# First loads of four stages spread over three DMA queues in a four-layer vision kernel

## The chip, the cores and the metric

The kernel runs on one core of a Trainium2 chip. The metric is the device time of one execution in microseconds. A core has a matrix engine (TensorE, PE in the profile), a vector engine (VectorE, DVE), a scalar engine (ScalarE, ACT), a general engine (GpSimd, POOL) and an engine that in this kernel only issues transfers (SyncE, SP). SP, ACT and POOL can each issue DMAs; a DMA that an engine issues stands in that engine's instruction order, so it waits for the instructions before it and holds up those behind it.

## The reference

Eight images of 56 by 56 pixels and 192 channels, in float32, pass through four residual layers. Each layer normalizes groups of channels and adds a sublayer's result:

```
x = x + L0(gn(x))   # gated Toeplitz mixing along rows and columns
x = x + L1(gn(x))   # attention in shifted 7x7 windows, 6 heads
x = x + L2(gn(x))   # 192 -> 384, 3x3 depthwise conv, four decaying
                    # running averages, layer norm, 384 -> 192
x = x + L3(gn(x))   # 7x7 depthwise conv, layer norm, MLP 192 -> 768 -> 192
```

Layer 1 rolls the image by three rows and three columns before it cuts it into windows, and rolls the result back. Layers 2 and 3 contain a depthwise convolution each, and every pixel of a channel plane is needed for them.

## The kernel before

The layers run one after the other, and between them the images lie in DRAM: x1[b] is image b after layer 0, x2[b] after layer 1. In SBUF an image has two halves of its rows on 64 partitions each, with three groups of 64 channels side by side.

**Layer 0** makes its gated products first and then mixes rows and columns (layer0_mix). It ends with a projection and a gate (L424 matmul, L429 activation, L445 matmul, L453 addition) and stores each image with L476, two DMAs on SP. When its mixing work is nearly through, it calls loaded(), which opens the pool l1x of layer 1's images (three buffers) and loads images 0 and 1.

**Layer 1** needs the image rolled. rolled() (L585 to L593) does the roll while loading: an image is cut into 18 DMAs, six pieces of rows and columns for each of the three channel groups. The large ones move rows of 53 pixels, 212 bytes, the small ones rows of three pixels, 12 bytes. The same function stores the finished image, rolled back, with 18 more. All are on SP. layer1_norm copies the image into windows and normalizes (ACT L614, PE L621, DVE L623 and following), layer1_scores and layer1_mix do the attention, and DVE's L762 adds the result into the image's own buffer, which is stored from there. Image b+2 is loaded in the middle of image b.

**Layer 2** begins with layer2_in, once per image: two memsets on POOL clear the border rows of the buffer x2 (L769, L770), two DMAs on SP bring the image's halves (L772, L773), DVE normalizes into xn (L778), two memsets on POOL clear xn's border (L781, L782), PE multiplies with w_in (L790), DVE adds b_in (L798), and the result pt goes to DRAM (pd, L799, SP). The pool l2x has two buffers for x2; they lie where layer 1's images lay. w_in and b_in are brought by POOL through the helper resident (L96).

layer2_mix then does the 3x3 convolution over all images at once, a group of channels at a time. For each group it loads a band of weights wt (L820) and one piece zc of every image's pd (L825), all on SP; PE's L834 needs them. convolve does the same for layer 3's 7x7 convolution (wt L997, zc L1002 from zd, PE L1009).

**What sets the order.** A planner orders the instructions of each engine. It goes by the order of the program as priority and by its own estimate of when an instruction can start, so a load may be placed on a queue far ahead of its place in the code if the queue is idle and its buffer is free, and behind one that comes later in the code. On the chip each engine then runs its instructions in that fixed order, and an instruction that waits holds up all behind it. A pool's buffers are used in turn; a new tile's first write waits for the last use of the memory.

Of the kernel before, what the change touches and what calls it, by code (L numbers as in the profile page):

```python
# [10 lines left out]
F32 = mybir.dt.float32  # L11
# [6 lines left out]
B, H, W, C = 8, 56, 56, 192  # L18
# [26 lines left out]
R2 = P2 + 1  # L45
# [31 lines left out]
def kernel(ctx: ExitStack, tc: tile.TileContext, a: dict, out: bass.AP):  # L77
    nc = tc.nc
    nimg = a["x"].shape[0]
# [14 lines left out]
    def resident(name, eng=nc.sync, pool=const):  # L94
        t = pool.tile(list(a[name].shape), F32, name=name + "_sb", bufs=1)
        eng.dma_start(t, a[name])  # L96
        return t
# [29 lines left out]
    x1 = [dram.tile([C, NT], F32, name=f"x1_{b}") for b in range(nimg)]  # L127
# [3 lines left out]
    zd = [dram.tile([OP, C, NB], F32, name=f"zd{b}") for b in range(nimg)]  # L131
# [3 lines left out]
    pd = [dram.tile([128, C2, P2], F32, name=f"pd{b}") for b in range(nimg)]  # L135
# [446 lines left out]
        nc.vector.tensor_scalar(wg[:, :, 0:C], wg[:, :, 0:C], HD ** -0.5, None, ALU.mult)  # L582
        return wg, bq, w_proj, bpr

    def rolled(dram_image, tile_image, store):  # L585

        d = dram_image.rearrange("(j p) (h w) -> p j h w", p=64, w=W)
        for s, h0, h1, r0 in ((0, 0, 28, 3), (1, 0, 25, 31), (1, 25, 28, 0)):
            for w0, w1, c0 in ((0, 53, 3), (53, 56, 0)):
                for j in range(3):  # L590
                    sb = tile_image[64 * s:64 * s + 64, j, h0:h1, w0:w1]
                    dr = d[:, j, r0:r0 + h1 - h0, c0:c0 + w1 - w0]
                    nc.sync.dma_start(dr, sb) if store else nc.sync.dma_start(sb, dr)  # L593

    def layer1_load(b, pool):
        x = pool.tile([128, 3, H // 2, W], F32, name="x1")
        rolled(x1[b], x, False)
        return x

    def layer1_norm(b, x, pool, psum, consts):  # L600
# [161 lines left out]
            nc.vector.scalar_tensor_tensor(xs, ps, bpr[:, j:j + 1], xs, ALU.add, ALU.add)  # L762


    def layer2_in(b, pool, xpool, psum, w_in, b_in):


        x = xpool.tile([128, 3, R2, W], F32, name="x2")
        nc.gpsimd.memset(x[0:64, :, 0], 0.0)  # L769
        nc.gpsimd.memset(x[64:128, :, R2 - 3:R2], 0.0)  # L770
        src = x2[b].rearrange("(j p) (h w) -> p j h w", p=64, w=W)
        nc.sync.dma_start(x[0:64, :, 1:R2], src[:, :, 0:R2 - 1])  # L772
        nc.sync.dma_start(x[64:128, :, 0:R2 - 3], src[:, :, R2 - 1:H])  # L773
        sc, sh = scsh2[:, b, 0], scsh2[:, b, 1]
        xn = pool.tile([128, 3, R2, 64], F32, name="xn2")
        nc.gpsimd.memset(xn[:, :, :, W:64], 0.0)
        for j in range(3):
            nc.vector.tensor_scalar(  # L778
                xn[:, j, :, 0:W], x[:, j], sc[:, j:j + 1], sh[:, j:j + 1], ALU.mult, ALU.add
            )  # L780
        nc.gpsimd.memset(xn[0:64, :, 0, 0:W], 0.0)  # L781
        nc.gpsimd.memset(xn[64:128, :, R2 - 3:R2, 0:W], 0.0)  # L782
        pt = pool.tile([128, C2, P2], F32, name="pt")
        nh = R2 // 2
        for i in range(nh):
            ns = 2 if i + nh < P2 else 1
            ps = psum.tile([128, 2, 512], F32, name="pin")
            for j in range(3):
                for s in range(ns):
                    nc.tensor.matmul(  # L790
                        ps[:, s, 0:C2], xn[64 * s:64 * s + 64, j, 2 * i:2 * i + 2].rearrange("p h w -> p (h w)"),
                        w_in[64 * s:64 * s + 64, j], start=(j == 0), stop=(j == 2),
                    )

            v = 0 if i == 0 else 2 if i + nh == P2 - 1 else 1
            dims = [list(z) for z in pt.ap]
            dst = bass.AP(pt.tensor, pt.offset + i, [dims[0], [nh, ns], [P2, C2]])
            nc.vector.tensor_tensor(dst, ps[:, 0:ns, 0:C2], b_in[:, v, 0:ns], ALU.add)  # L798
        nc.sync.dma_start(pd[b], pt)  # L799

    def layer2_mix():
# [5 lines left out]
        with ExitStack() as st:  # L807
            pool = st.enter_context(tc.tile_pool(reuse_waits="tile", name="mx", bufs=2))
# [8 lines left out]
            def load(g):  # L817
                cs = slice(g * CG2, (g + 1) * CG2)
                wt = pool.tile([128, CG2, 256], F32, name="wt2")
                nc.sync.dma_start(  # L820
                    wt, bass.AP(band.tensor, band.offset + g * CG2 * BL2, [[1, 128], [BL2, CG2], [1, 256]])
                )
                zc = pool.tile([128, nimg, CG2, P2], F32, name="zc2")
                for b in range(nimg):
                    nc.sync.dma_start(zc[:, b], pd[b][:, cs])  # L825
                return wt, zc

            def front(c4, wt, zc, loc, rows, sums):
# [159 lines left out]
    def convolve():  # L988

        band = a["band"]  # L990
        with ExitStack() as st:
            pool = st.enter_context(tc.tile_pool(reuse_waits="tile", name="cv", bufs=2))
            psum = st.enter_context(tc.tile_pool(reuse_waits="tile", name="cvp", bufs=3, space=PSUM))
            for g in range(C // CG):
                cs = slice(g * CG, g * CG + CG)
                wt = pool.tile([OP, CG, BAND], F32, name="wt")
                nc.sync.dma_start(  # L997
                    wt, bass.AP(band.tensor, band.offset + g * CG * BL, [[1, OP], [BL, CG], [1, BAND]])
                )
                zc = pool.tile([OP, nimg, CG, NB], F32, name="zc")  # L1000
                for b in range(nimg):
                    nc.sync.dma_start(zc[:, b], zd[b][:, cs])  # L1002
                yc = pool.tile([OP, nimg, CG, NPAIR], F32, name="yc")
                for c4 in range(0, CG, 4):
                    ps = psum.tile([OP, 2, 512], F32, name="cps")
                    for i in range(4):
                        dst = ps[:, i // 2, 256 * (i % 2):256 * (i % 2) + nimg * NPAIR]
                        for q in range(4):
                            nc.tensor.matmul(  # L1009
                                dst.rearrange("p (b n) -> p b n", n=NPAIR),  # L1010
                                wt[:, c4 + i, q * OP:(q + 1) * OP], zc[:, :, c4 + i, q:q + NPAIR],
                                start=(q == 0), stop=(q == 3),
                            )
                    for j in range(2):
                        src = ps[:, j].rearrange("p (i z) -> p i z", i=2)[:, :, 0:nimg * NPAIR]
                        src = src.rearrange("p i (b n) -> p b i n", n=NPAIR)
                        dst = yc[:, :, c4 + 2 * j:c4 + 2 * j + 2]
                        if j == 0:
                            nc.vector.tensor_copy(dst, src)
                        else:  # L1020
                            nc.scalar.copy(dst, src)
                for b in range(nimg):
                    nc.sync.dma_start(yd[b][:, cs], yc[:, b])
# [94 lines left out]
    with ExitStack() as st:  # L1118
# [6 lines left out]
        x = layer0_load(0, pool)  # L1125
# [28 lines left out]
    with ExitStack() as st:  # L1154
        pool = st.enter_context(tc.tile_pool(reuse_waits="tile", name="mix", bufs=2))
        psum = st.enter_context(tc.tile_pool(reuse_waits="tile", name="mixp", bufs=2, space=PSUM))
        w_p = resident("w_p", nc.gpsimd, pool)
        w_o = resident("w_o", nc.gpsimd, pool)

        ops = [psum.tile([128, 8, H], F32, name=f"op{k}", bufs=1) for k in range(2)]  # L1160
        for op in ops:
            nc.vector.memset(op, 0.0)
        images, x = ExitStack(), []

        def loaded():
            raws.close()
            xpool = images.enter_context(tc.tile_pool(reuse_waits="tile", name="l1x", bufs=3, side="right"))
            x.append(xpool)
            x.extend(layer1_load(b, xpool) for b in range(min(2, nimg)))

        layer0_mix(pool, blocks, psum, ops, w_p, w_o, loaded)


    with ExitStack() as st:
# [22 lines left out]
        xr = [next(steps)]  # L1197
        for _ in steps:
            pass
        values = layer1_scores(0, xr[0], pool, psum, S, es, consts)  # L1200


# [37 lines left out]
    with ExitStack() as st:  # L1240
        xpool = st.enter_context(tc.tile_pool(reuse_waits="tile", name="l2x", bufs=2, side="right"))
        pool = st.enter_context(tc.tile_pool(reuse_waits="tile", name="l2i", bufs=2))
        psum = st.enter_context(tc.tile_pool(reuse_waits="tile", name="l2ip", bufs=4, space=PSUM))
        w_in = resident("w_in", nc.gpsimd, pool)
        b_in = resident("b_in", nc.gpsimd, pool)
        for b in range(nimg):
            layer2_in(b, pool, xpool, psum, w_in, b_in)
            if b == nimg - 3:
                run(gn_finish(mv2[:, last], scsh2[:, last, 0], scsh2[:, last, 1], pool, psum, "pin"))
    layer2_mix()  # L1250
# [168 lines left out]
```

## Time and profile before

| | us |
|---|---|
| median of 3 runs | 6330.82 (6327.23 to 6345.44) |
| profiled execution | 6351.08 |
| its span | 6349.2 |
| PE busy in it | 5569.1 (88%) |
| DVE busy | 3439.3 (54%) |
| ACT busy | 2239.7 (35%) |
| POOL busy | 1302.1 (21%) |
| PE idle before layer 1's first matmul (L621) | 22.01 |
| PE idle before layer 2's first matmul (L790) | 55.65 |
| PE idle before layer 2's convolution (L834) | 27.89 |
| PE idle before layer 3's convolution (L1009) | 22.48 |

All durations come from the one profiled execution. In the lines of a timeline the first number is the start in microseconds from the beginning of the span, the second the time taken; then come the engine, the line of the code, the operation, the tile written and the tiles read, and how many instructions the row sums up. In brackets stands how long the engine had been idle before, and what released it. "SPq" rows are DMA issues on SP: their time is the time at the queue, not that of the transfer. q1 is the queue of SP, q0 that of POOL.

### The profile page before, as it was taken

What the parts mean: (1) busy time and instruction counts of PE and PEld (TensorE: products, weight loads), DVE (VectorE), ACT (ScalarE), POOL (GpSimd) and SP (SyncE); (2) the same over time, 40 slices, a digit from 0 to 9 for tenths busy, and PEclk for the clock granted to TensorE, in tenths of its full rate; (3) what the DMA queues carried; (4) which work ended last, traced back from release to release, by engine and by line L of the source; (5) the groups of instructions that cost most, each with busy time, mean ns of one, the idle gap of its engine ahead of it and who ended that gap; (6) DMA issues with size and microseconds to landing.
All of it is one profiled execution on the core that took longest, in us unless ns stands there. A gap on an engine that the chain in (4) does not pass through costs nothing. (4 is left out here: it accounts for less than half of the span.)

```text
span 6349.2 us, 126376 instructions
## 1 busy us (share of the span) xinstructions
PE 5569.1 (88%) x55636; PEld 3587.9 (57%) x55636; DVE 3439.3 (54%) x4752; ACT 2239.7 (35%) x2922; POOL 1302.1 (21%) x813
## 2 busy tenths in 40 slices
PE   6799989999999688888888598999588798789999
PEld 5677766666666345545445375777244498344444
DVE  5677765555665344444444486888688511532321
ACT  2334444443344233333332102555355300333333
POOL 1100034544444122122121102333110100110100
PEclk8899999999999888888888799999798799899999
DMA  6799886666665613444433675666667488121211
GB/s 166 185 221 210 188 262 263 260 253 240 240 252 194 88 33 55 60 58 63 55 48 44 103 266 208 224 228 233 153 203 208 170 305 305 64 67 56 70 54 27
DMA packets 1039131, 1013.10 MB, mean 160 GB/s; under 512 B 832104, under 2 KB 964372, under 8 KB 1011572
## 3 DMA queue, kind: packets, MB, share of 16 engines
q1 hardware_dynamic: 1028064, 954.17, 53.7%
q0 software_dynamic: 5648, 31.32, 1.5%
q10 hardware_dynamic: 4868, 19.52, 0.9%
q8 instruction: 437, 7.16, 0.5%
q14 instruction: 114, 0.93, 0.0%
HBM read 676.28 MB, written 345.08 MB: 161 GB/s over the span
## 5 line engine op out<-in xcount | busy, mean ns | idle before, releaser
L366 PE MATMUL qv<-w_qv_sb,xn 64*112 64x288 f32 x5376 | 722.2, 425 | 50.9 <-DVE act L372 47.6
L404 POOL COPY lc<-lt 128x896 f32<-128x896 f32 (+1 forms) x320 | 573.0, 1808 | 616.7 <-PE op L412 598.7
L366 PEld LDWEIGHTS qv<-w_qv_sb,xn 64*112 64x112 f32 x5376 | 535.5, 184 | 232.8 <-DVE act L372 64.7
L1087 PE MATMUL ph<-y,w_sb 64*128 64x392 f32 x2304 | 429.9, 511 | 49.1 <-ACT hid L1091 49.1
L373 ACT ACTIVATE act<-act 112x576 f32<-112x576 f32 x448 | 299.5, 682 | 461.7 <-DVE act L372 428.2
L1098 PE MATMUL po<-hid,w_sb 128*64 128x392 f32 x2304 | 395.1, 496 | 10.8 <-ACT hid L1091 10.8
L412 PEld LDWEIGHTS op<-rc,lc 128*56 128x56 f32 x9216 | 308.4, 136 | 127.6 <-issue 65.7
L412 PE MATMUL op<-rc,lc 128*56 128x56 f32 x9216 | 339.7, 222 | 46.0 <-POOL lc L404 24.2
L424 PE MATMUL pj<-xn,w_p_sb 64*128 64x392 f32 (+1 forms) x1920 | 373.0, 515 | 7.7 <-issue 4.7
L445 PE MATMUL y<-pp,w_o_sb 128*64 128x392 f32 (+1 forms) x1920 | 355.9, 503 | 20.4 <-DVE x L453 11.6
L372 DVE TENSOR_TENSOR act<-qv,b_qv 112x576 f32<-112x576 f32 x448 | 320.8, 751 | 86.1 <-PE qv L366 85.7
L1105 DVE TENSOR_TENSOR x<-x,z 128x392 f32<-128x392 f32 x96 | 55.8, 581 | 557.9 <-ACT z L1103 557.9
L1087 PEld LDWEIGHTS ph<-y,w_sb 64*128 64x128 f32 x2304 | 230.5, 194 | 224.1 <-ACT hid L1091 55.2
L404 ACT COPY rc<-rt 128x896 f32<-128x896 f32 (+1 forms) x160 | 256.9, 1606 | 230.7 <-PE op L412 216.0
L834 PE MATMUL cv<-zc,wt 128*128 128x224 f32 x1536 | 312.8, 355 | 27.9 <-DMA zc<-pd 27.9
L834 PEld LDWEIGHTS cv<-zc,wt 128*128 128x128 f32 x1536 | 290.5, 189 | 71.0 <-issue 54.9
L705 POOL TENSOR_TENSOR e<-e,mx 128x1176 f32<-128x1176 f32 x64 | 139.9, 2186 | 925.1 <-DVE mx L704 874.4
L655 PE MATMUL qk_ps<-xr,wg 64*96 64x392 f32 x1536 | 309.6, 511 | 14.9 <-ACT qk L661 13.3
L438 DVE TENSOR_TENSOR pp<-pp,ot 128x784 f32<-128x784 f32 (+1 forms) x160 | 154.6, 967 | 308.4 <-ACT pp L429 287.2
L1009 PE MATMUL cps<-zc,wt 128*128 128x224 f32 x1536 | 299.3, 356 | 23.1 <-DMA zc<-zd 22.5
L1009 PEld LDWEIGHTS cps<-zc,wt 128*128 128x128 f32 x1536 | 290.0, 189 | 32.5 <-issue 24.9
L847 POOL TENSOR_TENSOR rows<-rows,loc 128x896 f32<-128x896 f32 x96 | 228.1, 2377 | 390.2 <-ACT rows L843 262.8
(206 smaller groups left out, 9321.5 us busy)
## 6 DMA issues: line engine op xcount, KB each, us to landing
lt<-left SPq DMA_DIRECT2D x72, 1792.0 KB
rt<-right SPq DMA_DIRECT2D x72, 1792.0 KB
left<-qv SPq DMA_DIRECT2D x224, 252.0 KB
right<-qv SPq DMA_DIRECT2D x448, 126.0 KB
wt<-in_band_dram SPq DMA_DIRECT2D x24, 2048.0 KB
wt<-in_band_dram SPq DMA_DIRECT2D x12, 4096.0 KB
pd<-pt SPq DMA_DIRECT2D x8, 5568.0 KB
zc<-pd SPq DMA_DIRECT2D x192, 232.0 KB
```

The source lines that it names most:

```text
L366: nc.tensor.matmul(ps[s][:, which, 0:D1 // 2], xn[64 * s:64 * s + 64, j, bass.ts(i, 2 * W)], w_qv[64 * s:64 * s + 64, j, which, ns], start ...
L372: nc.vector.tensor_tensor(act, ps[s][:, :, 0:D1 // 2], b_qv[:, :, ns], ALU.add)
L373: nc.scalar.activation(act, act, AF.Silu)
L404: copy(c[:, 0:nu], raw.rearrange("p (w u d) -> p u d w", u=nu, d=64 // nu)[:, :, d0:d0 + 8])
L412: nc.tensor.matmul(op[64 * u:64 * u + W, i, :], lc[:, u, i], rc[:, u, i], start=True, stop=True)
L424: nc.tensor.matmul(ps[0:M, s, 0:TT], w_p[64 * s:64 * s + 64, j, d0:d0 + M], xn[64 * s:64 * s + 64, j, ts], start=(j == 0), stop=(j == 2),)
L445: nc.tensor.matmul(y[64 * s:64 * s + 64], w_o[0:M, c, 64 * j:64 * j + 64], pp[0:M, s], start=(c == gated[0][0]), stop=(c == gated[-1][0]),)
L655: nc.tensor.matmul(ps[s], wg[64 * s:64 * s + 64, j, c0:c0 + HC], xw[64 * s:64 * s + 64, j, gs], start=(j == 0), stop=(j == 2),)
L834: nc.tensor.matmul(dst, wt[:, c4 + i, 128 * q:128 * q + 128], zc[:, :, c4 + i, q:q + NPAIR], start=(q == 0), stop=(q == 1),)
L1009: nc.tensor.matmul(dst.rearrange("p (b n) -> p b n", n=NPAIR), wt[:, c4 + i, q * OP:(q + 1) * OP], zc[:, :, c4 + i, q:q + NPAIR], start=(q ...
L1087: nc.tensor.matmul(ps[:, s, 0:TT], w0[64 * s:64 * s + 64, j, m * 128:(m + 1) * 128], y[64 * s:64 * s + 64, j, ts], start=(j == 0), stop=(j ...
L1098: nc.tensor.matmul(ps[64 * s:64 * s + 64], w1[:, m, 64 * j:64 * j + 64], hid[:, m, s], start=(m == 0), stop=(m == 5),)
```

## The change

rolled and layer1_load take a list of queues and deal the channel groups out over them; layer 1's image 0 uses SP, POOL and ACT, six DMAs each. Image 1 is loaded from a place in the program after image 0's normalization. The first part of layer2_in becomes layer2_image(b, xpool, queue), called one image ahead: image 0's two halves go through POOL, the others through SP. w_in and b_in go through ACT, and image 0's load stands before them. In layer2_mix and convolve, the eight zc pieces of the first group go through SP, POOL and ACT in turn, those of the later groups through SP as before. One more tile of the pool l1x is asked for before image 0's (with eight images, -8 % 3 is 1), and nothing reads or writes it.

```diff
-    def rolled(dram_image, tile_image, store):
+    def rolled(dram_image, tile_image, store, queues=(nc.sync,)):
...
                 for j in range(3):
+                    eng = queues[j % len(queues)]
...
-                    nc.sync.dma_start(dr, sb) if store else nc.sync.dma_start(sb, dr)
+                    eng.dma_start(dr, sb) if store else eng.dma_start(sb, dr)
...
-    def layer2_in(b, pool, xpool, psum, w_in, b_in):
-
+    def layer2_image(b, xpool, queue):
         x = xpool.tile([128, 3, R2, W], F32, name="x2")
         nc.gpsimd.memset(x[0:64, :, 0], 0.0)
         nc.gpsimd.memset(x[64:128, :, R2 - 3:R2], 0.0)
         src = x2[b].rearrange("(j p) (h w) -> p j h w", p=64, w=W)
-        nc.sync.dma_start(x[0:64, :, 1:R2], src[:, :, 0:R2 - 1])
-        nc.sync.dma_start(x[64:128, :, 0:R2 - 3], src[:, :, R2 - 1:H])
+        queue.dma_start(x[0:64, :, 1:R2], src[:, :, 0:R2 - 1])
+        queue.dma_start(x[64:128, :, 0:R2 - 3], src[:, :, R2 - 1:H])
+        return x
+
+    def layer2_in(b, x, pool, psum, w_in, b_in):
...
                 zc = pool.tile([128, nimg, CG2, P2], F32, name="zc2")
+                queues = (nc.sync,) if g else (nc.sync, nc.gpsimd, nc.scalar)
                 for b in range(nimg):
-                    nc.sync.dma_start(zc[:, b], pd[b][:, cs])
+                    queues[b % len(queues)].dma_start(zc[:, b], pd[b][:, cs])
...
-            x.extend(layer1_load(b, xpool) for b in range(min(2, nimg)))
+
+            for _ in range(-nimg % 3):
+                xpool.tile([128, 3, H // 2, W], F32, name="x1")
+            x.append(layer1_load(0, xpool, (nc.sync, nc.gpsimd, nc.scalar)))
...
         xr = [next(steps)]
         for _ in steps:
             pass
+        if nimg > 1:
+            x.append(layer1_load(1, xpool))
         values = layer1_scores(0, xr[0], pool, psum, S, es, consts)
...
-        w_in = resident("w_in", nc.gpsimd, pool)
-        b_in = resident("b_in", nc.gpsimd, pool)
+        x = [layer2_image(0, xpool, nc.gpsimd)]
+        w_in = resident("w_in", nc.scalar, pool)
+        b_in = resident("b_in", nc.scalar, pool)
         for b in range(nimg):
-            layer2_in(b, pool, xpool, psum, w_in, b_in)
+            if b + 1 < nimg:
+                x.append(layer2_image(b + 1, xpool, nc.sync))
+            layer2_in(b, x[b], pool, psum, w_in, b_in)
```

convolve is changed like layer2_mix.

More of the change, by code (lines that the diff above doesn't have):

```diff
@@ L590, in rolled, with layer1_load @@
                 for j in range(3):
+                    eng = queues[j % len(queues)]
                     sb = tile_image[64 * s:64 * s + 64, j, h0:h1, w0:w1]
                     dr = d[:, j, r0:r0 + h1 - h0, c0:c0 + w1 - w0]
-                    nc.sync.dma_start(dr, sb) if store else nc.sync.dma_start(sb, dr)
-    def layer1_load(b, pool):
+                    eng.dma_start(dr, sb) if store else eng.dma_start(sb, dr)
+    def layer1_load(b, pool, queues=(nc.sync,)):
         x = pool.tile([128, 3, H // 2, W], F32, name="x1")
-        rolled(x1[b], x, False)
+        rolled(x1[b], x, False, queues)
         return x
@@ L1000, in convolve @@
                 zc = pool.tile([OP, nimg, CG, NB], F32, name="zc")
+                queues = (nc.sync,) if g else (nc.sync, nc.gpsimd, nc.scalar)
                 for b in range(nimg):
-                    nc.sync.dma_start(zc[:, b], zd[b][:, cs])
+                    queues[b % len(queues)].dma_start(zc[:, b], zd[b][:, cs])
                 yc = pool.tile([OP, nimg, CG, NPAIR], F32, name="yc")
```

## The prediction

> **What bounds the kernel now.** I read the page first, then the order of work on each queue around the four places that the diff touches, then the DMA engines in the same windows. In the page, TensorE (PE) is busy for 88% of the span:
>
> ```profile
> span 6349.2 us, 126376 instructions
> PE 5569.1 (88%) x55636; PEld 3587.9 (57%) x55636; DVE 3439.3 (54%) x4752; ACT 2239.7 (35%) x2922; POOL 1302.1 (21%) x813
> ```
>
> A change to loads can only win back time in which PE stands. In PE's timeline (start, length, line, tile, count, and in brackets the idle time before and what ended it) the four places are these four gaps:
>
> ```profile
> 2127.05 3.61 PE L621 MATMUL mean<-xr,ones 128*128 128x392 f32 x5 [22.01 <-issue]
> ...
> 3613.33 2.29 PE L790 MATMUL pin<-w_in_sb,xn 64*128 64x384 f32 x6 [55.65 <-POOL xn L781]
> ...
> 3884.49 1.83 PE L834 MATMUL cv<-zc,wt 128*128 128x224 f32 x4 [27.89 <-DMA zc<-pd]
> ...
> 5071.99 1.46 PE L1009 MATMUL cps<-zc,wt 128*128 128x224 f32 x3 [22.48 <-DMA zc<-zd]
> ```
>
> I call them A (into layer 1), B (into layer 2), C and D (first group of each convolution). Together 22.0 + 55.7 + 27.9 + 22.5 = 128 us, 2.0% of the span: the ceiling of the change. What fills A and B is seen in SP's queue:
>
> ```profile
> 2058.78 53.81 SPq L593 DMA_DIRECT2D x<-x  x36
> 2112.69 1.24 SPq L476 DMA_DIRECT2D x<-x  x2
> 2113.98 2.62 SPq L593 DMA_DIRECT2D x<-x  x1
> ...
> 3555.74 38.40 SPq L593 DMA_DIRECT2D x<-x  x18
> 3594.68 0.59 SPq L772 DMA_DIRECT2D x<-x  x1
> 3596.91 0.59 SPq L773 DMA_DIRECT2D x<-x  x1
> 3598.85 0.57 SPq L772 DMA_DIRECT2D x<-x  x1
> ```
>
> and in what the other engines wait for:
>
> ```profile
> 2126.21 5.83 ACT L614 ACTIVATE xr<-x,scsh 128x392 f32<-128x392 f32 x9 [33.01 <-DMA x<-x]
> 2126.22 2.69 POOL L1192 MEMSET e<- 128x1536 f32 x2 [24.77 <-DMA x<-x]
> ...
> 3560.57 0.26 POOL L769 MEMSET x<- 64x168 f32 x1
> 3598.84 0.23 POOL L769 MEMSET x<- 64x168 f32 x1 [37.45 <-DMA x<-x]
> 3609.71 3.28 DVE L778 TENSOR_SCALAR xn<-x,scsh 128x1680 f32<-128x1680 f32 x3 [50.34 <-DMA x<-x]
> 3613.05 0.23 POOL L781 MEMSET xn<- 64x168 f32 x1 [13.43 <-DVE xn L778]
> ```
>
> In A, ACT and POOL, which share nothing but reused memory, are released in the same moment, 12.3 us after the L476 store's last issue (2113.93): what they wait for is the store of layer 0's last image, not image 0's load. That store was ready about 2099, when DVE had made its last values, and stood behind 36 loads of images 0 and 1. In B the chain is: 18 stores of image 7, the two halves of layer 2's image 0, DVE, POOL's small memset L781, PE. The two L769 lines matter most: x2(0)'s memset did not wait, x2(1)'s waited 37.45 us for image 7's stores. So image 7 already lies outside layer 2's first buffer and inside its second.
>
> **Is it issue or bandwidth?** The DMA engines between 2058 and 2113 (busy tenths in 40 slices, then packets), and the first queue's share between 3857 and 3885 (C):
>
> ```profile
> DMA  0399999669999998723179999989999999994932
> ...
> DMA packets 43554, 5.97 MB, mean 109 GB/s; under 512 B 43374, under 2 KB 43374, under 8 KB 43550
> q1 hardware_dynamic: 43326, 4.82, 88.6%
> ...
> q1 hardware_dynamic: 3884, 10.24, 97.2%
> ```
>
> A moves slowly (109 GB/s) but its engines are full of packets under 512 B; C runs at 370 GB/s on full engines. D (5051 to 5072) likewise gave 361 GB/s at 100.5%, and B's stores 89.3% with 11.0% for b_in.
>
> **What the Trainium skill says.** The page "DMA: Bandwidth & Descriptors", section "Issuing engines are not separate DMA queues", says that DMAs begun on SP, ACT or GpSimd run on the same 16 engines and interleave, and that several issuers save only sequencer time; the shares above agree. Its section "SWDGE vs HWDGE vs iDMA" says that each engine takes turns between its queues; the trace agrees in B, where b_in on POOL's queue landed 9.9 us after its issue while the older stores nearly stood. "Rules for kernel authors" says that two halves of the partitions use the same engines and serialize: so x2's two halves are costed as one transfer.
>
> **Part A.** Image 0's 18 loads become 6 each on SP, POOL and ACT; image 1's are written after layer 1's first normalization, behind the store in program order. But the planner issues on an idle queue whatever is ready: in the trace SP issued image 2's first load at 2113.98, though the code has it half an image later. I therefore expect SP to carry 6 loads, image 1's 18 and one or so of image 2 before the store is ready. One load costs 53.81 / 36 = 1.49 us on average, a large one (1,792 rows; 24 ns for such a packet, over 16 engines) 2.7 us. Removed: the issue-bound ends, six small loads per image at 0.61 us, of which perhaps half finds other traffic: 2 x 3.7 / 2 = 3.7 us. Added: one large load, 2.7 us. Gain 1.0 us, taken. Ends: if image 1's loads do stay behind, the store starts between 2100 and 2107 and lands 13 us later, so ACT begins 5 to 13 us sooner; if three or four of image 2 slip ahead, 5 us are lost. ACT's 6 issues stand among the gate's L429 activations, which feed PE; the trace has no DMA of ACT there. At 1.49 us they cost 9 us of ACT, hidden while the last values arrive before the store's turn, 2112.7 against 2099: cover 13.7 us. At the largest issue on SP (5.6 us) they would take 34 us, and then A is lost by about 10. I take nothing. POOL is idle from 2058.75 to 2092.55, which covers its 6 issues unless they take over 34 us; the nearest rows, POOL issues of 49 to 384 descriptors, took 0.53 to 0.76 us.
>
> **Part B.** Layer 2's image 0 is written first and loads from POOL's queue; w_in and b_in move to ACT, image 1 stays on SP behind the stores. POOL reached x2(0)'s memset at 3560.57, after L776, whose memory comes free with DVE's last L762 (3558.5); I expect the same, since x2(0)'s and x2(1)'s memsets were queued one after the other, as if all of layer 1's buffers came free at once. The load then starts at about 3561 among the stores. It is 2.35 MB in 384 packets of 515 ns: 384 x 515 / 16 = 12.4 us of all engines. DVE's 3 x 3.28 = 9.8 us could follow at about 3575. But POOL is in order: x2(1)'s two memsets, waiting for image 7's stores, stand ahead of L781 and L782, which wait for DVE, and PE waits for L781. So PE starts when the stores have landed: 3598.84 + 12.4 (full engines, x2(0) served among them) + 0.75 (x2(1)'s memsets) + 0.3 (L781) = 3612.3, against 3613.33: 1.0 us gained. The stores' last, smallest transfers may leave gaps that take some of the 12.4, so I take 2. Ends: nothing absorbed and w_in (0.59 MB, at C's 370 GB/s 1.6 us) moved among the stores, loss 1; half of 12.4 absorbed, gain 7. Image 1 does not add a stall: its load lands about 14 us after the stores, plus 9.8 of DVE, within image 0's 30.5 us on PE.
>
> **Part C and D.** C moves, in turn, the pd store (14.1 us), the weights (5.9) and eight zc (5.3), all of which PE's first matmul needs, at 97.2% of the engines: three issuers change their order and not the sum. SP's blocked issue (20.98 us for eight) only waited for the pd store. Gain 0; ends -2 (the second group's weights, no longer held back by SP, share the engines with the last zc) and +1. D: weights 10.8 us and zc 5.6 at 100.5%; only the first 3 us (5051.4 to 5054.9) could start sooner. I take 0.5; ends 0 and 3.
>
> **The unread tile.** One extra tile per three images shifts the order of layer 1's buffers, if a tile that nothing reads or writes counts at all. I take it as without effect: image 7 stays where the L769 lines show it.
>
> **Sum.** 1.0 + 2.0 + 0 + 0.5 = 3.5 us less in a profiled execution of 6351.08 us (span 6349.2), which lay 20.3 above the median of the runs; the same difference against the median gives 6330.8 - 3.5 = 6327.3 us. No change under 0.3% (19 us) can be told from none in this kernel.
>
> **Rivals.** *First, the waits really go* (chance 0.37). If L781 stands ahead of x2(1)'s memsets, PE starts at about 3585, computes image 0 in 30.5 us, and then waits for image 1 (stores 3611, load 13, DVE 9.8, so 3634) where it would have begun at 3643.8: 10 gained, up to 20 if x2(0) starts before the stores. With A's 5 to 13: 6330.8 - (15 + 8 + 0.5) = 6307, down to 6290. For it: DVE idles 50 us and nothing but queue order holds L781. Against it: in this trace x2(1)'s and x2(2)'s memsets come before the later L781. *Second, slower* (0.18): the extra tile does count and puts image 7 into x2(0)'s buffer. Then x2(0)'s memset waits for the stores (3598.8); its load is issued at 3600 and shares the engines with x2(1)'s, landing after 2 + 12.4 to 2 + 24.8 us; with 9.8 of DVE and 0.3, PE starts between 3624.5 and 3637, a loss of 11 to 24, time 6342 to 6355, taken as 6349. It decides from a landing at 3622 on. For it: three buffers, and layer 2's first is as wide as one and a bit. Against: nothing uses the tile. *Third, ACT's issues block the gate* (0.07): PE's last layer 0 work ends 10 us later, 6338. *The change hardly does what it says* is the forecast itself (0.38): the bytes and the in-order wait remain.
>
> **Numbers.** Forecast 0.38 at 6327, its own range 6316 to 6340, nearly all within 0.3%. First rival 0.37, of which 0.32 is over 19 us. Second 0.18, of which 0.13 over. Third 0.07, of which 0.03. With 0.01 from the forecast's own ends on each side: faster 0.33, slower 0.17, same 0.50. The range goes from 6292, near the first rival's end, to 6348, and leaves out about a tenth on each side.
>
> **What would show it.** A: on SP some 24 loads ahead of L476, ACT's first L614 at 2120 to 2128. B: x2(0)'s load issued by POOL near 3561, DVE's first L778 near 3575, yet L781 only after a L769 that waits for image 7, near 3611. C and D: the gaps 27.9 and 22.5 within 3 us. Wrong: L781 before that L769, or L476 issued before 2107 (faster); a waiting first L769, or ACT's L429 apart by issues (slower).

## The result, and the profile after

The change makes the kernel slower by a little: 6350.5 us (median of 13 runs) against 6330.8, a ratio of 1.0033 with a 95% interval of 1.0022 to 1.0045. Measured once more later, beside the kernel before on one chip, it was 6352.4 against 6340.6, ratio 1.0019 (1.0011 to 1.0027). So the loss lies near 12 to 20 us. The forecast was 6327.3 us, and its range ended at 6348.

The profiled execution of the change has a span of 6344.6 us, which is shorter than that of the kernel before (6349.2): stages that the change does not touch differ from one execution to the next by as much as the loss. So I compare the stages and not the spans. PE's timeline of the changed kernel, at the four places of the prediction (start, length, line, tile, count, idle time before and what ended it; lines have moved by 1 to 6):

```profile
2122.01 4.26 PE L622 MATMUL mean<-xr,ones 128*128 128x392 f32 x6 [7.92 <-issue]
...
3616.18 24.25 PE L794 MATMUL pin<-w_in_sb,xn 64*128 64x384 f32 x132 [66.87 <-POOL xn L785]
...
3887.56 2.95 PE L839 MATMUL cv<-zc,wt 128*128 128x224 f32 x7 [28.54 <-DMA zc<-pd]
...
5071.72 8.53 PE L1015 MATMUL cps<-zc,wt 128*128 128x224 f32 x33 [20.30 <-DMA zc<-zd]
```

B has grown from 55.65 us to 66.87, by 11.2. C is 0.6 longer, D 2.2 shorter. A seems to have shrunk from 22.0 to 7.9, but that is no gain. PE's last work of layer 0 has moved back. Here are the last gate activation of ACT ahead of layer 1's loads and PE's last row of layer 0, in the kernel before and in the changed one:

```profile
2056.09 0.92 ACT L429 ACTIVATE pp<-pj,vecs_sb 128x784 f32<-128x784 f32 x1 [2.46 <-PE pj L424]
2094.25 2.42 PE L445 MATMUL y<-pp,w_o_sb 64*64 64x392 f32 x12 [1.21 <-DVE pp L438]
...
2048.36 0.92 ACT L429 ACTIVATE pp<-pj,vecs_sb 128x784 f32<-128x784 f32 x1 [2.46 <-PE pj L424]
2102.47 3.98 PE L445 MATMUL y<-pp,w_o_sb 64*64 64x392 f32 x12 [1.21 <-DVE pp L438]
```

ACT's timeline of the changed kernel shows why PE is later ("ACTq" rows are DMA issues on ACT, with the time for which they held it):

```profile
2051.07 10.25 ACTq L594 DMA_DIRECT2D x<-x  x3
2061.43 0.91 ACT L429 ACTIVATE pp<-pj,vecs_sb 128x784 f32<-128x784 f32 x1 [10.93 <-issue]
2061.45 6.05 ACTq L594 DMA_DIRECT2D x<-x  x1
...
2068.55 5.30 ACTq L594 DMA_DIRECT2D x<-x  x2
```

Six issues held ACT for 21.6 us between the gate's activations, which feed PE. The L429 among them is the line to look at: its 10.93 us of idle time end with "issue", not with a result of PE. From one and the same L429 activation, the last one ahead of the loads (2056.09 before, 2048.36 after; called the common L429 below), to PE's first matmul of layer 1 it took 70.96 us before and takes 73.65 now. So A costs 2.7 us more. SP in the meantime:

```profile
2051.06 48.10 SPq L594 DMA_DIRECT2D x<-x  x26
2107.09 1.25 SPq L476 DMA_DIRECT2D x<-x  x2
```

SP was through with 26 loads at 2099.2 and then stood still until the store of layer 0's last image was ready, at 2107.1. Together the four places give 2.7 + 11.2 + 0.6 - 2.2 = 12.3 us.

Layer 2's start holds most of the loss. The queues of SP, POOL and DVE in the changed kernel, and of POOL's two transfers the time from issue to landing (last number, us):

```profile
3547.36 45.94 SPq L594 DMA_DIRECT2D x<-x  x18
3596.02 0.59 SPq L772 DMA_DIRECT2D x<-x  x1
...
3543.92 0.23 POOL L769 MEMSET x<- 64x168 f32 x1
...
3544.67 0.67 POOL L772 DMA_DIRECT2D x<-x  x1
...
3596.12 0.23 POOL L769 MEMSET x<- 64x168 f32 x1 [50.15 <-DMA x<-x]
...
3614.95 1.18 POOL L785 MEMSET xn<- 64x168 f32 x1 [18.04 <-DVE xn L782]
...
3610.54 6.48 DVE L782 TENSOR_SCALAR xn<-x,scsh 128x1680 f32<-128x1680 f32 x6 [59.55 <-DMA x<-x]
```

```profile
x<-x POOLq DMA_DIRECT2D x1, 1218.0 KB, 10.8
...
x<-x POOLq DMA_DIRECT2D x1, 1134.0 KB, 18.5
```

Image 0's halves were issued at 3544.67 and 3545.33 and had landed by 3563.8. Still DVE did nothing until 3610.54, and then ran six normalizations in a row, those of image 0 and of image 1. What came at 3610.5 is image 1's load, issued at 3596.0 behind the stores. In the program's order on DVE, one of image 1's three normalizations stands ahead of image 0's. The lines show it: POOL's L785 waits for image 0's three and was released at 3614.95, when four of the six were done (3610.54 + 4 x 6.48 / 6 = 3614.86). DVE is in order as POOL is: it waited with image 0 ready for 47 us.

### The profile page after: what moved, and what is told of

It is laid out like the page before. It is cut to its first block, busy times and chain, and to the rows that moved or that the text cites. A ratio compares the mean times of both kernels' runs of the same rounds, so it can differ in the third digit from the quotient of the medians.

```text
span 6344.6 us, 126393 instructions
## 1 busy us (share of the span) xinstructions
PE 5564.0 (88%) x55636; PEld 3581.2 (56%) x55636; DVE 3434.6 (54%) x4752; ACT 2239.3 (35%) x2922; POOL 1312.0 (21%) x825
## 5 line engine op out<-in xcount | busy, mean ns | idle before, releaser
L445 PE MATMUL y<-pp,w_o_sb 128*64 128x392 f32 (+1 forms) x1920 | 361.3, 508 | 25.7 <-DVE x L453 11.6
L1015 PE MATMUL cps<-zc,wt 128*128 128x224 f32 x1536 | 298.9, 356 | 20.5 <-DMA zc<-zd 20.3
```

The costliest lines, as they stand in the source:

```text
L445: nc.tensor.matmul(y[64 * s:64 * s + 64], w_o[0:M, c, 64 * j:64 * j + 64], pp[0:M, s], start=(c == gated[0][0]), stop=(c == gated[-1][0]),)
L1015: nc.tensor.matmul(dst.rearrange("p (b n) -> p b n", n=NPAIR), wt[:, c4 + i, q * OP:(q + 1) * OP], zc[:, :, c4 + i, q:q + NPAIR], start=(q ...
```

## The experiments

### Each part alone

Three kernels take one part of the change each, and leave the rest as in the kernel before. The times that the expectations name are counted from the first 6330.8 us; in the comparisons that follow, the kernel before had medians of 6336 to 6342 us, so the differences and ratios are what to compare.

```diff
# a_only: layer 1's loads as in the change; layer 2 as before, and
-  queues = (nc.sync,) if g else (nc.sync, nc.gpsimd, nc.scalar)
+  queues = (nc.sync,)
# b_only: layer 2's loads as in the change, the others as before
# cd_only: the two zc lines as in the change, the others as before
```

> Layer 1's first loads alone: image 0 over three queues, image 1 behind the first normalization, the rest as in the kernel before. Theory: ACT's six issues block for some 20 us between the gate's activations, so PE's last work of layer 0 ends about 15 us later, while SP reaches the store 7 us sooner; PE's first matmul of layer 1 comes 0 to 3 us later, counted from the first load: 6331 to 6335 us. Rival (the missing 10 us of the whole sit here, as a slower layer 1 or a lower clock after the longer gate): 6339 to 6345 us.

> Layer 2's first loads alone: image 0 on POOL's queue, w_in and b_in on ACT's, image 1 on SP's. Theory: DVE has one instruction of image 1 ahead of image 0's, so PE waits for image 1's load: gap of 66 to 68 us before layer 2's first matmul against 55.7, 6340 to 6344 us. Rival (the loss of the whole lies elsewhere): gap as before, 6329 to 6333 us.

> The first loads of both convolutions over three queues, the rest as in the kernel before. Theory: the transfers are limited by the DMA engines; gaps of 28 and 20 to 22 us, 6328 to 6332 us. Rival (three queues at once make the engines slower): gaps longer by 5 us and more, 6336 to 6345 us.

Measured against the kernel before: a_only ratio 1.0007 (0.9999 to 1.0014), about +4 us; from the common L429 to layer 1's first matmul 73.7 us against 71.0. b_only 1.0017 (1.0007 to 1.0026), about +11 us, with a gap of 67.8 us. cd_only 0.9994 (0.9984 to 1.0004), about -4 us and not told from nothing, with gaps of 27.8 and 20.5 us. PE's first matmul of layer 2 in b_only:

```profile
3621.96 38.36 PE L794 MATMUL pin<-w_in_sb,xn 64*128 64x384 f32 x218 [67.78 <-POOL xn L785]
```

The part of layer 2 is most of the loss, as its gap says. A gap alone does not tell what a stage costs, since it also shrinks when the work before it ends late: A's gap is 7.6 us in a_only and 22.0 before, and the kernel is not faster.

### Does the issue on ACT stall the gate?

```diff
-            x.append(layer1_load(0, xpool, (nc.sync, nc.gpsimd, nc.scalar)))
+            x.append(layer1_load(0, xpool, (nc.sync, nc.gpsimd)))
```

on top of a_only.

> Layer 1's first loads alone, as before in this series, but image 0 is dealt out over SP and POOL only, none to ACT. Theory (ACT's blocked issues stall the gate): the gate ends on time, SP is through with its loads about 7 us sooner than in the kernel before, so PE's first matmul of layer 1 comes 5 to 9 us sooner, counted from the first load: 5 to 9 us less than before. Rival (the small descriptors on POOL's queue hold up the engines): no gain against the three-queue form, 0 to 5 us more than before.

Measured: 0.9983 (0.9972 to 0.9994), about 11 us less than before. The stretch from the common L429 to layer 1's first matmul is 62.8 us, 8.2 less than before and 11 less than with ACT. SP and PE:

```profile
2044.00 44.45 SPq L594 DMA_DIRECT2D x<-x  x22
2088.55 5.19 SPq L476 DMA_DIRECT2D x<-x  x2
```

```profile
2104.07 4.26 PE L622 MATMUL mean<-xr,ones 128*128 128x392 f32 x6 [13.89 <-issue]
```

Of image 0's loads, SP has twelve here and POOL six. The store follows directly on the loads before it, of which there are 22 on SP, since eight of image 1's now come after it. POOL's six issues (5.4 us) cost PE nothing; six like them on ACT cost it the gain. The two forms differ in these eight loads too, but in the change SP stood free for 7.9 us ahead of the store, so most of the 11 us between them is put down to ACT's stall.

### Is it the store's place in the queue?

The kernel before, with one line of store() changed, used for the last image:

```diff
+            queue = nc.scalar if b == nimg - 1 else nc.sync
             for s in range(2):
-                nc.sync.dma_start(
+                queue.dma_start(
```

> The kernel before with one change: the store of layer 0's last image is issued by ACT, not by SP behind the 36 loads. Theory (it is the store's place in SP's queue that holds layer 1 back): the store is issued near its readiness, 12 us sooner, its large packets take turns with the small ones, and PE's gap into layer 1 falls from 22 us to 9 to 13: 9 to 13 us less than before. Rival (the engines are full, so the place in the queue does not matter): gap of 19 us and more, 0 to 3 us less.

Measured: 0.9971 (0.9962 to 0.9980), about 18 us less than before, with nothing else of the change in it. SP, ACT and PE of that kernel:

```profile
2055.47 63.29 SPq L595 DMA_DIRECT2D x<-x  x37
```

```profile
2094.00 1.36 ACTq L477 DMA_DIRECT2D x<-x  x2
```

```profile
2109.21 4.26 PE L623 MATMUL mean<-xr,ones 128*128 128x392 f32 x6 [7.51 <-issue]
```

The loads' issues now take until 2118.8, and layer 1 begins 9.6 us before that. The store was issued at 2094.0 and had landed by 2108.4, when POOL was released. The DMA engines were full then as before: from 2094 to 2109, ACT's queue, which held only the store, had 64.0% of them and SP's queue of loads 33.8%. So the place in a queue does matter: on a queue of its own the store took turns with the loads instead of standing behind all of them. Counted from the common L429 it was issued after 41.2 us instead of 56.6, and the whole stretch is 56.4 us against 71.0, a little more gain than the theory's 9 to 13.

### What holds DVE, and what holds POOL?

First try: image 0 of layer 2 issued by ACT instead of POOL, on top of b_only.

```diff
-        x = [layer2_image(0, xpool, nc.gpsimd)]
+        x = [layer2_image(0, xpool, nc.scalar)]
```

> As the run with layer 2's first loads alone, but image 0's two halves are issued by ACT instead of POOL, behind w_in and b_in. The planner then puts image 0's three normalizations first on DVE. Theory (DVE's order is what costs): PE then waits only for POOL's L769, that is for image 7's stores: gap of 49 to 53 us, about 15 us less than with POOL, 6324 to 6330 us. Rival (the load's traffic among the stores is what costs): gap of 65 us and more, 6340 to 6345 us.

Measured: 1.0007 (0.9997 to 1.0016), gap 54.8 us. Neither gap came out. DVE's order was right (image 0's three first), but the load was late. ACT's queue:

```profile
3561.15 0.37 ACTq L96 DMA_DIRECT2D b_in_sb<-in_b_in_dram  x1
3593.93 0.69 ACTq L772 DMA_DIRECT2D x<-x  x1
3596.03 0.61 ACTq L773 DMA_DIRECT2D x<-x  x1
```

The load stood 32 us at the head of ACT's queue, and went out as the last of SP's 18 stores were issued (to 3594.4). In the trace this wait ends with the landing of one of SP's stores, whose completion is counted by the same semaphore as the load's; SP's and ACT's transfers use one set of semaphores in turn in this program. That the load had to wait until the semaphore's last user had landed is the likely cause; I did not try it apart. So this run does not decide between the two theories.

Second try: image 1 goes through POOL's queue as well, behind image 0.

```diff
-                x.append(layer2_image(b + 1, xpool, nc.sync))
+                x.append(layer2_image(b + 1, xpool, nc.sync if b else nc.gpsimd))
```

> Layer 2's first loads alone, with images 0 and 1 both on POOL's queue. The planner then has image 0's three normalizations first on DVE. Theory: DVE is done early and PE waits for POOL alone, whose L785 stands behind the memset and the issues of image 1, that is behind image 7's stores: gap of 49 to 52 us, 4 to 7 us less than before. Rival (the traffic among the stores costs as much as the order): gap of 56 us and more, no gain.

Measured: 1.0019 (1.0011 to 1.0027), about 12 us more than before. In the groups of instructions (busy time, mean ns | idle time before, by releaser):

```profile
L794 PE MATMUL pin<-w_in_sb,xn 64*128 64x384 f32 x1392 | 241.9, 498 | 65.5 <-POOL xn L785 52.7 <-DVE pt L802 12.8
```

The first gap is 52.7 us, near what was expected. A second of 12.8 us has come. SP had sent image 2's load at 3599.01, since image 2 takes image 0's buffer, and POOL sent image 1's at 3605.20, so that the later image moved first. DVE, in order, waited with image 0's additions behind image 1's normalization.

The same with image 0's border left out, so that nothing on POOL follows its normalization:

```diff
+        if b == 0:
+            nc.gpsimd.memset(xn[0:64, :, 0, 0:W], 0.0)
+            nc.gpsimd.memset(xn[64:128, :, R2 - 3:R2, 0:W], 0.0)
         for j in range(3):
+            parts = ((0, 64, 1, R2), (64, 128, 0, R2 - 3)) if b == 0 else ((0, 128, 0, R2),)
+            for p0, p1, r0, r1 in parts:   # tensor_scalar on these rows
...
+        if b:
             nc.gpsimd.memset(xn[0:64, :, 0, 0:W], 0.0)
```

> As the run before it, and image 0's normalization leaves out xn's border rows, which POOL clears beforehand, so that nothing of POOL follows DVE for image 0 (six half instructions of DVE in place of three). Theory: both in-order waits are gone; PE starts 20 to 24 us after layer 1's end, then waits 12 to 18 us for image 1: 15 to 20 us less than before. Rival (the image's load does not land among the stores): first gap of 40 us and more, at most 5 us less.

Measured: 1.0010 (1.0000 to 1.0019), no gain (the interval reaches from none to 12 us more). PE and DVE of that kernel:

```profile
3558.07 5.46 PE L801 MATMUL pin<-w_in_sb,xn 64*128 64x384 f32 x8 [9.91 <-DVE xn L787]
3566.36 19.36 PE L801 MATMUL pin<-w_in_sb,xn 64*128 64x384 f32 x88 [2.83 <-DVE xn L787]
3624.88 25.51 PE L801 MATMUL pin<-w_in_sb,xn 64*128 64x384 f32 x134 [39.17 <-DVE pt L809]
```

```profile
3620.11 3.29 DVE L787 TENSOR_SCALAR xn<-x,scsh 128x1680 f32<-128x1680 f32 x3 [40.56 <-DMA x<-x]
```

PE starts 9.9 us after layer 1's end and not 20 to 24: the load does land among the stores. But image 1's normalization stands on DVE ahead of eleven of image 0's fifteen additions (L809), which empty PE's buffers, and PE stops for 39 us after about half of image 0. The wait of B is found a third time in another place.

### DVE's order alone

The cleanest way to take image 1 off DVE is to let ACT, idle in this stage, normalize it. The first kernel does only that to b_only, the second has image 0's border left out as well.

```diff
         for j in range(3):
+            if b == 1:
+                nc.scalar.activation(
+                    xn[:, j, :, 0:W], x[:, j], AF.Identity, bias=sh[:, j:j + 1], scale=sc[:, j:j + 1]
+                )
+                continue
```

> Layer 2's first loads alone (image 0 on POOL, image 1 on SP, as in the change), but image 1 is normalized by ACT, which is idle there, so that none of its instructions stand on DVE. Theory: DVE does image 0 near 15 us after layer 1's end and PE then waits for POOL's L785 behind image 1's memset, that is for image 7's stores alone: gap of 48 to 52 us, 4 to 8 us less than before, 15 us less than with image 1 on DVE. Rival (the early traffic is what costs): gap of 60 us and more.

> As the run before it, and image 0's normalization leaves out xn's border rows, which POOL clears beforehand. Theory: no in-order wait is left for image 0; PE starts 10 to 20 us after layer 1's end, works for image 0, and waits again, until image 1 has landed 15 us after image 7's stores: 10 to 16 us less than before. Rival (the early start is given back wholly while PE waits for image 1): within 3 us of before.

b_norm: 0.9991 (0.9981 to 1.0000), about 6 us less than before and about 17 less than b_only. DVE, POOL and PE:

```profile
3565.64 3.29 DVE L787 TENSOR_SCALAR xn<-x,scsh 128x1680 f32<-128x1680 f32 x3 [12.11 <-DMA x<-x]
```

```profile
3598.34 0.23 POOL L769 MEMSET x<- 64x168 f32 x1 [49.80 <-DMA x<-x]
...
3599.19 0.23 POOL L790 MEMSET xn<- 64x168 f32 x1
```

```profile
3599.47 40.94 PE L799 MATMUL pin<-w_in_sb,xn 64*128 64x384 f32 x236 [47.63 <-POOL xn L790]
```

This is the picture of the prediction: DVE done at 3569, POOL's memset for image 0 behind that of image 1, PE 1.1 us after the stores. It needed DVE's order to be other than in the change. The early load is the same in b_only, so the load is not what cost there.

b_norm_split: 0.9973 (0.9963 to 0.9983), about 17 us less than before. PE:

```profile
3558.70 5.46 PE L806 MATMUL pin<-w_in_sb,xn 64*128 64x384 f32 x8 [10.06 <-DVE xn L792]
3566.54 31.76 PE L806 MATMUL pin<-w_in_sb,xn 64*128 64x384 f32 x166 [2.38 <-DVE xn L792]
3616.52 10.08 PE L806 MATMUL pin<-w_in_sb,xn 64*128 64x384 f32 x48 [18.22 <-POOL xn L797]
```

Image 0 is worked off while the stores still move, and PE then waits 18.2 us for image 1. Image 1 begins 67.9 us after layer 1's end (3548.6); before, it was 55.65 + 30.5 = 86.2 us. So the load on POOL's queue does bring what it was meant to bring, when neither DVE nor POOL holds it up.

### A version that beats both

best_a is a_store with the convolutions' loads on three queues; best_c also has layer 2 as in b_norm_split. Layer 1 loads as before.

> The kernel before with the store of layer 0's last image issued by ACT, and with the convolutions' first loads on three queues as in the change; layers 1 and 2 load as before. Theory (the two are apart in time and add up): 16 to 22 us less than before. Rival (the convolutions' part is worth nothing): 13 to 18 us less.

> Both fixes and the convolutions' part together: the store of layer 0's last image on ACT, layer 1 loading as before; layer 2's image 0 on POOL without border memsets behind its normalization, image 1 normalized by ACT; the convolutions' first loads on three queues. Theory (gaps far apart add up): 17 to 18 us from each, 30 to 38 us less than before. Rival (what one wins the other gives back, through a lower clock): 15 to 25 us less.

best_a: 0.9974 (0.9965 to 0.9984), no better than a_store alone; the convolutions' part is worth too little to be seen in the whole. best_c: 6312.1 us against 6340.6, 0.9948 (0.9929 to 0.9967), about 33 us less than before. In the trace the two gains stand side by side: the stretch into layer 1 is 56.3 us (56.4 in a_store), and PE's gap ahead of image 0 is 9.55 us (10.06 in b_norm_split). In the time of the whole they add up as far as six runs tell: the interval reaches from 21 to 45 us, so the rival's 25 is not excluded. Its group of layer 2 and of layer 1's first matmuls:

```profile
L807 PE MATMUL pin<-w_in_sb,xn 64*128 64x384 f32 x1392 | 244.7, 496 | 32.0 <-POOL xn L798 18.5 <-DVE xn L793 12.4 <-DVE pt L815 0.8
...
L623 PE MATMUL mean<-xr,ones 128*128 128x392 f32 x192 | 76.6, 535 | 8.5 <-issue 7.6 <-ACT xr L616 0.9
```

### Do the parts add up?

The three parts alone gave 4 + 11 - 4 = 11 us, the first comparison of the whole 21.

> The change as it is, once more beside the kernel before. Theory (the parts add up): 4 + 11 - 4, that is 5 to 17 us more than before. Rival (the whole costs more than its parts): 20 us and more.

Measured: ratio 1.0019 (1.0011 to 1.0027), 12 us (7 to 17), which is the sum of the parts and of the stages in the trace. Its gaps are those of the first profile (67.2 us in B, 28.3 and 20.8 in C and D). Why the first comparison was higher is not settled; the intervals overlap.

## Why the prediction was wrong

**Part B, the step "POOL is in order ... So PE starts when the stores have landed".** This step failed. It followed POOL's order to its end and took DVE's for granted ("DVE's 3 x 3.28 = 9.8 us could follow at about 3575"). One instruction of image 1 ahead of image 0's on DVE made PE wait for image 1's load, which came 14.5 us after the stores, and not for the stores: a gap of 66.9 us, 11.2 more than before, where the step had 1.0 less. b_norm, with that instruction off DVE, started PE 47.6 us after layer 1, where the change took 66.9. With two images loading at once through two queues, the order of their users is open on every engine behind them, not only on the one where the trace of before shows a wait; that is what the step left out.

**A misread row in the same sum.** "3 x 3.28" took the time of a row as that of one instruction. The row's time is that of all three: 3609.71 + 3.28 = 3612.99 meets L781 at 3613.05. DVE's part was a third of what I wrote. It did not decide here, since DVE was taken as hidden, but it made the first rival's gain for B, 10 us, too small by 6.5: with both waits gone, image 1 began 18 us earlier in b_norm_split.

**The stores' delay.** The prediction added 12.4 us of traffic to the stores' landing and took about 1 us of it as absorbed. From first issue to landing it was 43.1 us before and 48.8 in the change (3547.36 to 3596.12): 5.6 of 12.4 us were seen. This term was too large, as the upper end had it (half absorbed). With the right size the step would have given a gain of some 8 us, which is what b_norm shows in its gap (47.6 against 55.65). That "the older stores nearly stood" was also too strong a reading: while b_in landed in the kernel before (3558.8 to 3568.7), POOL's queue had 50.1% of the engines and SP's stores 47.5%. That x2's halves serialize agrees with the change, where they landed one after the other, 10.8 and 18.5 us after their issue.

**Part A, the step "I take nothing" for ACT's issues.** I gave two values, 9 us at the average issue and 34 at the largest, and a cover of 13.7 us. The six issues took 21.6 us, and PE's last layer 0 work came 17.5 us later by the common L429 (L445's last row ends 58.1 us after it, against 40.6). Cover and cost nearly met: 2.7 us lost in place of 1.0 gained. The third rival was this mechanism; its price was put too high. The planner did put image 1's loads ahead of the store, and the order was nearly as forecast: 26 loads on SP (by number and size 6 of image 0, 18 of image 1 and two of image 2), then L476. SP was through with them 48.1 us after the first, where the store had waited 53.9 us before; so without ACT's stall some 5.8 us were to be had, and a_noact, with 22 loads ahead of the store on SP, got 8.2 from the common L429. The gain of 1.0 was thus too small, and which term of its sum was off is not separated. The sum also put the store behind every transfer, whatever queue it was in; a_store showed that a store on a queue of its own does not stand behind the loads.

**Parts C and D.** Right: +0.6 and -2.2 us, inside the ends given. D's 2 us come back in each of the five traces with three queues (gaps of 20.3 to 20.8 us, against 22.4 to 22.9 in the others), but in the time of the whole they can't be told from nothing.

**The unread tile.** Right: x2(0)'s L769 ran at 3543.92 without waiting, as it did in b_only without the tile, so image 7 does not lie in layer 2's first buffer. The second rival, which was the only one on the slower side with weight, did not happen. Most of the loss came from a place that none of the rivals named.

**The limit of 0.3%.** It was too coarse: with 13 and more runs of each kernel the intervals are 5 to 7 us to each side, and gains of 11 us and losses of 12 could be told from none.

**What an issue costs.** The Trainium skill, page "DMA: Bandwidth & Descriptors", section "Issuing engines are not separate DMA queues", says that several issuers save only sequencer time, which is usually small beside the transfer. For the bytes that held: C moved by 0.6 us and D by 2.2. For an engine that also computes the sequencer's time was not small: 21.6 us for six issues on ACT, up to 1,792 short rows each, against 0.36 to 0.38 us each for w_in and b_in on ACT, which have 128 rows. And the order of completion did change with the queue (a_store, 18 us), though the sum of the bytes did not.

## What to carry to other kernels

When a load is moved to another queue, list on every engine behind it the order of the instructions that use it and of those that use the load's neighbours: each engine waits in order, and a wait that is freed on one is often found on the next. Do not issue many small-row transfers from an engine that has work between them that feeds the bottleneck (ACT here); try first to give a short, urgent transfer its own queue, which won about 18 us here, before moving the long, patient ones away from it, which won about 11 at best. And measure a gap from a common instruction ahead of it, since a gap also shrinks when the work before it comes late.

## What the runs showed of the hardware

Six transfers of 12- and 212-byte rows held ACT for 21.6 us in the change, and six like them, issued at the same time, POOL for 5.4 us (2053.07 to 2058.44). ACT's single issues took from 0.58 to 8.19 us. The first, of 1,792 rows, took 0.70 us, so the number of rows alone does not make an issue long; what does was not tried apart. Two transfers of 1.2 MB in large packets, put in beside 18 transfers of small rows that filled the engines, landed in 10.8 and 18.5 us, while the small ones took only 5.6 us longer in all. A small memset on POOL took 1.18 us instead of 0.23 (L785 in the change) while DVE ran its normalizations at the same time; in b_only it took 1.18 us likewise.
